# Next head's maxima and rows made in the middle of a head and carried through DRAM; routing in 16-bit floats with the gates kept in the gathered rows

## The chip, the cores and the metric

The kernel runs on one core of one Trainium2 chip. The metric is the time of one execution on the device in microseconds (us). Besides the span, which runs from the first to the last instruction of the profiled execution, there is the clock that TensorE was granted, as a share of full speed.

The core's engines work from queues of their own: TensorE (PE in the profile; PEld is its weight load), VectorE (DVE), ScalarE (ACT), GpSimd (POOL) and SyncE (SP, which issues most DMA transfers here). An engine takes its instructions in the order in which they stand in its queue. Semaphores order work between queues.

## The reference, cut to what matters

The input is 1250 nodes of 768 numbers and 41250 directed edges. Two blocks add to the input, each after a layer normalisation: the first is a graph network (two attention layers over the edges, and a linear combination) plus a linear attention (`mix`); the second is a mixture of eight experts, of which each node uses two.

```python
h = (x @ W).reshape(n, H, C)                      # layer 1: H=4, C=192; layer 2: H=2, C=96
s_src = (h * a_src).sum(-1); s_dst = (h * a_dst).sum(-1)
e = leaky_relu(s_src[src] + s_dst[dst], 0.2)
emax = segment_max(e, dst)
ee = exp(e - emax[dst])
alpha = ee / segment_sum(ee, dst)[dst]
out = segment_sum(alpha[:, :, None] * h[src], dst)
...
k = elu(x @ Wk + bk) + 1;  v = x @ Wv + bv        # mix, 12 heads of 64
kv = einsum('bhnd,bhne->bhde', k, v)              # and q likewise, then out @ Wo
...
gate = xt @ Wg + bg                               # 8 experts
scores, idx = top_k(gate, 2)
y = (gelu(xt @ W1[e] + b1[e])) @ W2[e] + b2[e]    # for each expert e
out = sum over a node's two experts of scores * y
```

## The kernel before, in words

Nodes are tiled as 10 tiles (NT) of 125 (PT). The edges are turned into a dense table `AT` of edge counts (source tile by destination) and a table `mask` of ones and zeros (destination tile by source). An attention head is then a dense job over 1250 x 1250 numbers.

**A head (`attend`, L496 to L538).** `ss` and `sd` are one column each of source and destination scores.

1. `across` (L498 to L508) turns a column of 10 x 125 scores into a row of 1250 that stands in all 125 partitions. It does ten TensorE transposes of a broadcast column (L504), four to a PSUM bank, and three ScalarE copies (L506). The first such row is `ss_row`, from which the least score of the head (`least`, L481 to L493) is taken off by the copy's bias, so that all entries are at least zero.
2. For each destination tile, one VectorE instruction multiplies `ss_row` with the mask and keeps the largest product (L515, `scr` and `top`): the largest neighbouring source score. Ten of these make a head's maxima.
3. L518 to L525 form from `top` the columns `up`, `dn` and `sl`. `up` and `dn` go through `across` to become `up_row` and `dn_row`.
4. For each source tile `st`, ScalarE takes two exponentials (L533 into `w`, L534 into `v`), VectorE takes the larger (L535) and limits and multiplies it with the edge counts (L536), and TensorE multiplies `w` with the features (`gather`): in layer 1 ten matmuls into `ag` (L548), in layer 2 three (L569). A matmul in 32-bit floats stands in the profile as two records.
5. In layer 1 the head ends with a reciprocal (L555) and ten VectorE instructions that add the scaled result into `h2` (L557). In layer 2 ScalarE copies the result out (L574). Layer 2 reads `h2`, so it begins when all four heads of layer 1 are added.

There are four heads in layer 1 and two in layer 2. The buffers that matter: three `w`, two `v`, one each of `ss_row`, `up_row` and `dn_row`, and one `ag`, which lies in five of the eight PSUM banks; `across` has one bank and the projection below has two.

**The key and value projection (L600 to L629)** depends on none of the heads. For each node tile and each half of 384 columns, there are six matmuls with Wk, six with Wv (L607), an exponential part on VectorE and ScalarE (L611 to L614), a copy (L617), three matmuls of keys by values (L621) and an addition to `kvacc` (L627, L629).

**What sets the order.** The kernel is written in a tile framework that schedules each engine's queue when the program is built: work that is ready by the framework's reckoning goes first in the order of the text, and later work fills the gaps. The order is fixed from then on. This is how the projection's matmuls come to stand between the heads' work on TensorE. The weights Wo, Wq and Wu (L584 to L591) take the place in memory of the graph's tables and so are loaded (L588, on SP) when the last head is done.

**Routing (L743 to L863).** For each node tile TensorE computes a query (L751), the sum of the linear parts (`po`, L781) and of the graph part (`u`, L792); VectorE adds and normalises (`xl`); the normalised row is written to `xl_d` in DRAM (L802); transposes and six matmuls give the eight gate values (L807, L810). VectorE ranks them (L817 to L826), two matmuls with a triangle and a matrix of ones count earlier nodes with the same expert (L830, reading `sel` and `cum`), and the result is a place in a list of 80 columns (NV) of 128 for each of the node's two experts. One-hot tables `hot` (L849) and `put` (L852, twice: node number and gate value) are multiplied into `inv` (L854), in 32-bit floats. At the end `idx` (node numbers, L859) and `gs` (gate values, L861) are read from `inv`.

**Experts (L899 to L984).** For each expert, three groups of 128 nodes are gathered from `xl_d` by an indirect DMA on GpSimd's queue (L909), transposed (L912, L915), passed through the two layers (L926, L938), scaled by the gates in `gs` (L942) and added to the output by an indirect DMA (L943). What does not fit in three groups follows in `other` (L959).

Of the kernel before, what the change touches and what calls it, by code (L numbers as in the profile page):

```python
# [54 lines left out]
FIX = 3  # L55
# [14 lines left out]
def gps_block(ctx: ExitStack, tc: tile.TileContext, x, src, dst, norm_g, norm_b, W1, a_src1, a_dst1,  # L70
# [60 lines left out]
    xl_d = dram.tile([N + 128, D], F32)  # L131
# [348 lines left out]
    def least(ss, H):  # L480

        mn = small.tile([PT, H], F32, name="mn")
        nc.vector.tensor_reduce(mn, ss.rearrange("p t h -> p h t"), AX.X, ALU.min)
        p = four()
        nc.tensor.transpose(p[:H, 0], mn, ident[:PT, :PT])
        m1 = small.tile([H, 1], F32, name="m1")
        nc.vector.tensor_reduce(m1, p[:H, 0], AX.X, ALU.min)
        p = four()
        nc.tensor.transpose(p[:, 0, :H], m1.to_broadcast([H, PT]), ident[:H, :H])
        lo = small.tile([PT, 2, H], F32, name="lo")  # L490
        nc.vector.tensor_copy(lo[:, 0], p[:, 0, :H])
        nc.vector.tensor_scalar(lo[:, 1], p[:, 0, :H], -1.0, None, op0=ALU.mult)
        return lo  # L493

    def attend(ss, sd, lo, wp, rb, gather):

        def across(cols, name, bufs, bias=0.0):

            row = rb.tile([PT, N], F32, name=name, bufs=bufs)
            for g0 in range(0, NT, 4):  # L500
                n = min(4, NT - g0)
                p = four()
                for q in range(n):
                    nc.tensor.transpose(p[:, q], cols[:, g0 + q:g0 + q + 1].to_broadcast([PT, PT]),  # L504
                                        ident[:PT, :PT])
                nc.scalar.activation(row[:, g0 * PT:(g0 + n) * PT],  # L506
                                     p[:, :n].rearrange("p a b -> p (a b)"), AF.Identity, bias=bias)
            return row  # L508


        ss_row = across(ss, "ss_row", 1, lo[:, 1:2])
        top = small.tile([PT, NT], F32, name="top")
        for t in range(NT):
            scr = wp.tile([PT, N], BF16, name="scr", bufs=1)
            nc.vector.tensor_tensor_reduce(scr, ss_row, mask[:, t], 1.0, 0.0, ALU.mult, ALU.max,  # L515
                                           top[:, t:t + 1])

        nc.vector.scalar_tensor_tensor(top, top, lo[:, 0:1], sd, op0=ALU.add, op1=ALU.add)  # L518
        nc.vector.scalar_tensor_tensor(top, top, SLOPE, top, op0=ALU.mult, op1=ALU.max)
        up = small.tile([PT, NT], F32, name="up")  # L520
        dn = small.tile([PT, NT], F32, name="dn")
        sl = small.tile([PT, NT], F32, name="sl")
        nc.vector.tensor_sub(up, sd, top)
        nc.vector.scalar_tensor_tensor(dn, sd, SLOPE, top, op0=ALU.mult, op1=ALU.subtract)
        nc.vector.tensor_scalar(sl, ss, SLOPE, None, op0=ALU.mult)  # L525
        up_row = across(up, "up_row", 1)
        dn_row = across(dn, "dn_row", 1)
        for st in range(NT):


            w = wp.tile([PT, N], F32, name="w", bufs=3)
            v = wp.tile([PT, N], F32, name="v", bufs=2)
            nc.scalar.activation(w, up_row, AF.Exp, bias=ss[:, st:st + 1])  # L533
            nc.scalar.activation(v, dn_row, AF.Exp, bias=sl[:, st:st + 1])  # L534
            nc.vector.tensor_tensor(w, v, w, op=ALU.max)  # L535
            nc.vector.scalar_tensor_tensor(w, w, 2.0, AT[:, st, :N], op0=ALU.min, op1=ALU.mult)  # L536
            gather(st, w)

    lo1 = least(s1[:, :, :, 0], H1)
    with tc.tile_pool(name="wp", bufs=3) as wp, tc.tile_pool(name="rb", bufs=1) as rb:  # L540
        with tc.tile_pool(name="ag_p1", bufs=1, space=PSUM) as ag_p:
            for hd in range(H1):
                ag = ag_p.tile([PT, NT // 2, 512], F32, name="ag")

                def gather1(st, w):
# [6 lines left out]
                attend(s1[:, :, hd, 0], s1[:, :, hd, 1], lo1[:, :, hd], wp, rb, gather1)  # L552
                v = ag[:, :, :2 * CG].rearrange("p a (b c) -> p a b c", b=2)
                rd = small.tile([PT, NT // 2, 2, 1], F32, name="rd")
                nc.vector.reciprocal(rd, v[:, :, :, C2:C2 + 1])  # L555
                for t in range(NT):
                    nc.vector.scalar_tensor_tensor(h2[:, t], v[:, t // 2, t % 2], rd[:, t // 2, t % 2],  # L557
                                                   h2[:, t], op0=ALU.mult, op1=ALU.add)
# [3 lines left out]
        lo2 = least(h2[:, :, at:at + H2], H2)  # L562
        with tc.tile_pool(name="ag_p2", bufs=1, space=PSUM) as ag_p:
            for hd in range(H2):
                ag = ag_p.tile([C2 + 1, 3, 512], F32, name="ag")

                def gather2(st, w):
# [4 lines left out]
                attend(h2[:, :, at + hd], h2[:, :, at + H2 + hd], lo2[:, :, hd], wp, rb, gather2)  # L572
                for i, (a, b) in enumerate(NCH):
                    nc.scalar.copy(o2T[:, hd, a:b], ag[:, i, :b - a])  # L574
# [23 lines left out]
    for t in range(NT):  # L598
        ky = kp.tile([PT, D], F32, name="ky", bufs=2)
        va = kp.tile([PT, KC, 129], F32, name="va")  # L600
        nc.gpsimd.memset(va[:, :, 128:], 1.0)
        for k in range(2):
            half = slice(k * 384, (k + 1) * 384)
            for w in (Wk_sb, Wv_sb):
# [4 lines left out]
                if w is Wk_sb:  # L609
                    ke = kp.tile([PT, 384], F32, name="ke", bufs=1)  # L610
                    nc.vector.tensor_add(ky[:, half], ps[:PT, :384], bk_b[:, half])  # L611
                    nc.vector.tensor_scalar(ke, ky[:, half], 0.0, None, op0=ALU.min)
                    nc.scalar.activation(ke, ke, AF.Exp)
                    nc.vector.scalar_tensor_tensor(ky[:, half], ky[:, half], 0.0, ke, op0=ALU.max,  # L614
# [5 lines left out]
            for c in range(3):  # L620
                nc.tensor.matmul(ps[:, c * 129:(c + 1) * 129],  # L621
                                 ky[:, (3 * k + c) * 128:(3 * k + c + 1) * 128], va[:, 3 * k + c],
# [63 lines left out]
    zero = fp.tile([128, D], F32)  # L686
    nc.gpsimd.memset(zero, 0.0)
    nc.sync.dma_start(xl_d[N:], zero)
    nc.sync.dma_start(out[N:], zero)
# [4 lines left out]
    gs = fp.tile([128, NV + 1], F32)  # L694
# [4 lines left out]
    with ExitStack() as rs:  # L699
# [7 lines left out]
        def numbers(shape, pattern, base, mult, name):  # L707
            t = rp.tile(shape, F32, name=name)
# [8 lines left out]
        row128 = numbers([PT, 128], [[1, 128]], 0, 0, "row128")  # L717
        steps = numbers([128, NE, NJ - FIX], [[0, NE], [128, NJ - FIX]], 128 * FIX, 0, "steps")
        slot_row = numbers([PT, NV], [[1, NV]], 0, 0, "slot_row")
# [6 lines left out]
        ones = rp.tile([PT, 128], F32)  # L726
        nc.gpsimd.memset(ones, 1.0)
        tri = rp.tile([PT, 128], F32)
# [4 lines left out]
        nc.gpsimd.memset(gs[:, NV:], 0.0)  # L733
# [5 lines left out]
        cum = rp.tile([PT, NT + 1, NE], F32)  # L739
        nc.vector.memset(cum[:, 0], 0.0)  # L740
        inv = g_p.tile([128, 2, NV], F32, name="inv", bufs=1)
# [26 lines left out]
        for t in range(NT):  # L768
# [30 lines left out]
            xl = rl.tile([PT, D], F32, name="xl")  # L799
            normalise(xl, xt)  # L800
            for p, tt in token_rows(t):
                nc.sync.dma_start(xlr[p, tt], xl[p])  # L802
# [6 lines left out]
            gate = rl.tile([PT, NE], F32, name="gate")  # L809
            nc.vector.tensor_add(gate, pg[:PT, :NE], bg_b)  # L810

# [11 lines left out]
            sel = rl.tile([PT, NE], F32, name="sel")  # L823
# [10 lines left out]
            two = rl.tile([PT, 2, 2, NE], F32, name="two")  # L834
            for i, a in enumerate((at, gate)):
                nc.vector.tensor_mul(two[:, i], kth, a[:, None, :].to_broadcast([PT, 2, NE]))
            both = rl.tile([PT, 2, 2], F32, name="both")
# [112 lines left out]
    for e in range(NE):  # L950
        hT = hidden(ring[e], xT, FIX, fb1T[:, :, e:e + 1])
        if e + 1 < NE:
            xT = gather([r for r, _ in fixed(e + 1)])
# [62 lines left out]
```

## Time and profile before

| | |
|---|---|
| time, median of 3 runs | 1179.41 us (1175.86 to 1180.65) |
| the profiled execution | 1180.66 us, span 1178.6 us |
| TensorE's granted clock over the span | 0.971 |
| busy: TensorE, weight load, VectorE, ScalarE, GpSimd | 1077.8, 723.6, 669.1, 358.1, 76.3 us |
| first L535 of layer 1, last L557 of layer 1 | 249.2 us, 466.2 us |
| first L535 of layer 2, last L569 | 503.0 us, 593.4 us |
| first L781 | 613.0 us |
| first gather (L909) | 937.5 us |

How the page is read. The busy time of an engine is the time in which one of its instructions ran. Matmuls are pipelined, so their time in the listing is longer than the distance between two of them. The chain is found by going back from the last instruction to what released it. A stretch of the span is shown as a line with its ends, its length, the busy time of each engine (with the number of instructions), the clock and the DMA engines' mean busy share and rate. A timeline shows merged instructions with start and duration, and in brackets the idle time before them and what ended it.

### The profile page before, as it was taken

The numbers are of one execution on the slowest core, as the hardware profiler recorded it, in microseconds if no ns is written. First come the engines' busy times: TensorE is split into PE (matmuls) and PEld (weight loads), VectorE is DVE, ScalarE is ACT, GpSimd is POOL, SyncE is SP. The second block draws the span as 40 slices with busy tenths as digits, with TensorE's granted clock in tenths as the row PEclk, the third lists the DMA queues.
The fourth block names the chain that finished last, engine by engine and source line by source line (L and its number), as shares of the span: only waits on it lengthen the run. The fifth ranks groups of instructions, "written<-read, shape, count | busy, mean of one in ns | idle before, by whom it ended". The sixth has DMA issues, their size and how long they took to land.

```text
span 1178.6 us, 12106 instructions
## 1 busy us (share of the span) xinstructions
PE 1077.8 (91%) x4583; PEld 723.6 (61%) x4583; DVE 669.1 (57%) x1366; ACT 358.1 (30%) x527; POOL 76.3 (6%) x100
## 2 busy tenths in 40 slices
PE   2599998999999999988989999999999589999993
PEld 2586655578788878544545666666666356666652
DVE  6866666669696966687922555555555422222210
ACT  2131114373737373373712211111111011111111
POOL 1000000000000000000000000000000122322321
PEclk9999998999999999989989999999999789999997
DMA  5014000000000001000083111111123537777533
GB/s 156 27 51 163 16 25 1 1 1 1 1 1 1 1 1 53 1 0 1 1 319 103 40 40 40 40 40 40 39 65 106 191 91 188 200 209 219 121 56 54
DMA packets 33282, 79.62 MB, mean 68 GB/s; under 512 B 5258, under 2 KB 13020, under 8 KB 33208
## 3 DMA queue, kind: packets, MB, share of 16 engines
q1 hardware_dynamic: 27608, 59.02, 15.2%
q0 software_dynamic: 5600, 19.66, 8.4%
q8 instruction: 40, 0.66, 0.2%
q14 instruction: 34, 0.28, 0.1%
HBM read 60.37 MB, written 18.30 MB: 67 GB/s over the span
## 4 chain that ended last, share of the span: by engine, by line
PE 70%; DVE 20%; DMA 5%; issue 2%; ACT 2%; POOL 1%; DVEq 0%; SPq 0%; POOLq 0%; ACTq 0%
PE po L781 13%; PE ph L926 8%; PE py L938 7%; PE mm L430 7%; PE mm L607 7%; PE mm L751 7%; DVE scr L515 6%; DVE w L535 5%; DVE w L536 5%; PE ag L548 3%; PE ag L569 2%; PE u L792 2%; PE px L912 2%; PE mm L405 2%; DMA w<-in_L_gnn_Wu_dram 2%
## 5 line engine op out<-in xcount | busy, mean ns | idle before, releaser
L548 PE MATMUL ag<-kept,w 125*125 125x198 f32 x800 | 137.4, 333 | 5.1 <-DVE w L536 4.9
L548 PEld LDWEIGHTS ag<-kept,w 125*125 125x125 f32 x800 | 133.5, 188 | 9.0 <-DVE w L536 9.0
L926 PE MATMUL ph<-xsT,w 128*128 128x384 f32 (+1 forms) x324 | 100.6, 470 | 1.8 <-DVE xsT L915 1.8
L938 PE MATMUL py<-w,hT 128*128 128x384 f32 x300 | 100.6, 486 | 0.0
L430 PE MATMUL mm<-Wg,xnT 128*125 128x400 f32 x240 | 91.8, 520 | 1.0 <-DVE xnT L321 0.6
L607 PE MATMUL mm<-Wv_sb,xnT 128*125 128x384 f32 x240 | 85.7, 489 | 4.8 <-DVE kvacc L627 4.8
L535 DVE TENSOR_TENSOR w<-v,w 125x1250 f32<-125x1250 f32 x60 | 86.3, 1453 | 6.6 <-ACT w L533 5.9
L515 DVE CUSTOM_DVE_ANT_0 scr<-ss_row,mask 125x1250 bf16<-125x1250 f32 x60 | 87.2, 1453 | 0.5 <-ACT ss_row L506 0.2
L781 PE MATMUL po<-w,xnT 128*125 128x384 f32 x240 | 84.8, 496 | 2.6 <-DMA w<-in_L_gnn_Wu_dram 2.6
L536 DVE SCALAR_TENSOR_TENSOR w<-w,AT 125x1250 f32<-125x1250 f32 x60 | 86.4, 1455 | 0.4
L926 PEld LDWEIGHTS ph<-xsT,w 128*128 128x128 f32 x324 | 59.8, 193 | 41.4 <-DVE xsT L915 2.4
L607 PE MATMUL mm<-Wk_sb,xnT 128*125 128x384 f32 x240 | 84.4, 486 | 0.0
L534 ACT ACTIVATE v<-dn_row,sl 125x1250 f32<-125x1250 f32 x60 | 79.3, 1333 | 16.9 <-DVE w L535 16.4
L751 PE MATMUL mm<-w,xnT 128*125 128x384 f32 x240 | 84.2, 489 | 0.0
L915 DVE COPY xsT<-px 128x384 f32<-128x384 f32 x50 | 25.5, 552 | 99.2 <-PE px L912 77.3
L781 PE MATMUL po<-w,qT 128*125 128x384 f32 x240 | 80.8, 486 | 0.0
L938 PEld LDWEIGHTS py<-w,hT 128*128 128x128 f32 x300 | 55.3, 190 | 33.9
L941 DVE TENSOR_TENSOR ys<-py,wb 128x768 f32<-128x768 f32 x25 | 23.9, 958 | 74.0 <-PE py L938 45.5
L781 PEld LDWEIGHTS po<-w,xnT 128*125 128x125 f32 x240 | 44.2, 190 | 30.1 <-DMA w<-in_L_gnn_Wu_dram 2.8
L781 PEld LDWEIGHTS po<-w,qT 128*125 128x125 f32 x240 | 44.2, 188 | 29.4
L607 PEld LDWEIGHTS mm<-Wv_sb,xnT 128*125 128x125 f32 x240 | 42.4, 187 | 31.1 <-DVE kvacc L627 6.9
L751 PEld LDWEIGHTS mm<-w,xnT 128*125 128x125 f32 x240 | 43.6, 188 | 27.6 <-ACT qT L321 0.2
(274 smaller groups left out, 1415.6 us busy)
## 6 DMA issues: line engine op xcount, KB each, us to landing
w<-in_L_ffn_W_dram SPq DMA_DIRECT2D x18, 1152.0 KB
xt<-in_x_dram SPq DMA_DIRECT2D x20, 336.0 KB
wb<-in_L_ffn_b_dram SPq DMA_DIRECT2D x9, 384.0 KB
out_dram<-xt SPq DMA_DIRECT2D x10, 336.0 KB
xl_d<-xl SPq DMA_DIRECT2D x10, 336.0 KB
W_sb<-in_L_gnn_W_dram SPq DMA_DIRECT2D x1, 2304.0 KB
Wk_sb<-in_L_mix_Wk_dram SPq DMA_DIRECT2D x1, 2304.0 KB
Wv_sb<-in_L_mix_Wv_dram SPq DMA_DIRECT2D x1, 2304.0 KB
```

Source lines behind the costliest of these rows:

```text
L430: nc.tensor.matmul(ps[:PT, :2 * (CG + 2)], xnT[:, c, t * PT:(t + 1) * PT], Wg1[:, c, 2 * k:2 * k + 2].rearrange("p h c -> p (h c)"), start ...
L515: nc.vector.tensor_tensor_reduce(scr, ss_row, mask[:, t], 1.0, 0.0, ALU.mult, ALU.max, top[:, t:t + 1])
L534: nc.scalar.activation(v, dn_row, AF.Exp, bias=sl[:, st:st + 1])
L535: nc.vector.tensor_tensor(w, v, w, op=ALU.max)
L536: nc.vector.scalar_tensor_tensor(w, w, 2.0, AT[:, st, :N], op0=ALU.min, op1=ALU.mult)
L548: nc.tensor.matmul(ag[:, t // 2, o:o + CG], w[:, t * PT:(t + 1) * PT], gw[:, st, hd], start=st == 0 and t % 2 == 0, stop=st == NT - 1, ski ...
L607: nc.tensor.matmul(ps[:PT, :384], xnT[:, c, t * PT:(t + 1) * PT], w[:, c, half], start=c == 0, stop=c == KC - 1)
L751: nc.tensor.matmul(ps[:PT, :384], xnT[:, c, tk], Wq_sb[:, c, half], start=c == 0, stop=c == KC - 1)
L781: nc.tensor.matmul(po[k][:, :384], l, r[:, k * 384:(k + 1) * 384], start=i == 0, stop=i == len(parts) - 1)
L915: nc.vector.tensor_copy(xT[:, 3 * a:3 * a + 3, j * 128:(j + 1) * 128], px[:, a, :384].rearrange("p (b n) -> p b n", b=3))
L926: nc.tensor.matmul(ph[:, :n * 128], w[0][:, o:o + 128], xT[:, c, :n * 128], start=c == 0, stop=c == KC - 1)
L938: nc.tensor.matmul(py[:, k, :384], hT[:, f, j * 128:(j + 1) * 128], w[:, o:o + 384], start=f == 0, stop=f == FC - 1)
```

## The change

*Attention.* `attend` becomes `layer`, which takes all heads of a layer. The least score of each head is subtracted from its column by VectorE (`over`), and the columns of all heads are turned by one transpose (`to_rows`), copied by ScalarE and written to DRAM. The rows of the layer's first head are still made by `across`; those of the other heads are read back from DRAM by a DMA that repeats a row in all 125 partitions. What was `up_row` and `dn_row` is one buffer `row` of two rows, of which there are two; `v` has one buffer instead of two. The call for the next head's `ss_row`, maxima and rows (`sides_of`) stands after the third source tile of a head instead of at the start of the next.

*Projection.* The buffer `ky` holds a half (384) instead of a whole tile, and there are three.

*Routing.* `row128`, `slot_row`, `ones`, `tri`, `cum`, `sel`, `hot` and `put` are 16-bit floats. `put` and `inv` hold node numbers alone, so that one L852 of two is left and `inv` has 80 columns instead of 160. The eight gate values of a node are kept as eight more columns of `xl`, and two more DMAs for each tile write them to `xl_d`, whose rows are 776 numbers long.

*Experts.* A gather brings the gates along, and the scaling reads them from the gathered row (`xg`, six buffers instead of three). In `other` the gate column is copied after the gather, by an address in a register.

```diff
+    row_d = [dram.tile([n * NT, PT], F32, name=f"row{i}") for i, n in enumerate((H1, H2, 2))]
-    xl_d = dram.tile([N + 128, D], F32)
+    xl_d = dram.tile([N + 128, D + NE], F32)
...
-        ss_row = across(ss, "ss_row", 1, lo[:, 1:2])
...
+    def to_rows(cols, d):
+        n = cols.shape[1]
+        p = four()
+        nc.tensor.transpose(p[:n, 0], cols, ident[:PT, :PT])
+        r = small.tile([H1 * NT, PT], F32, name="r", bufs=2)
+        nc.scalar.copy(r[:n], p[:n, 0])
+        nc.sync.dma_start(d, r[:n])
...
+    def layer(ss, sd, H, d, wp, rb, head):
+        lo = least(ss, H)
+        over = small.tile([PT, H, NT], F32, name="over", bufs=1)
+        for h in range(H):
+            nc.vector.tensor_scalar(over[:, h], ss[:, :, h], lo[:, h:h + 1], None, op0=ALU.subtract)
+        to_rows(over.rearrange("p h t -> p (h t)"), d)
+        def sides_of(h):
+            ss_row = rb.tile([PT, N], F32, name="ss_row")
+            if h:
+                nc.sync.dma_start(ss_row, row_bcast(d[h * NT:(h + 1) * NT], PT))
+            else:
+                across(over[:, h], ss_row)
...
+            row = rb.tile([PT, 2, N], F32, name="row", bufs=2)
+            if h:
+                to_rows(sides.rearrange("p a t -> p (a t)"), row_d[2])
+                nc.sync.dma_start(row.rearrange("p a n -> p (a n)"), row_bcast(row_d[2], PT))
+            else:
+                for a in range(2):
+                    across(sides[:, a], row[:, a])
+            return row, sl
+        ahead = sides_of(0)
+        for h in range(H):
+            row, sl = ahead
+            gather, finish = head(h)
+            for st in range(NT):
+                if st == 3 and h + 1 < H:
+                    ahead = sides_of(h + 1)
+                w = wp.tile([PT, N], F32, name="w", bufs=3)
+                v = wp.tile([PT, N], F32, name="v", bufs=1)
...
-        ky = kp.tile([PT, D], F32, name="ky", bufs=2)
+                    ky = kp.tile([PT, 384], F32, name="ky", bufs=3)
...
-        ones = rp.tile([PT, 128], F32)
+        ones = rp.tile([PT, 128], F16)
...
-        inv = g_p.tile([128, 2, NV], F32, name="inv", bufs=1)
+        inv = g_p.tile([128, NV], F32, name="inv", bufs=1)
...
-            xl = rl.tile([PT, D], F32, name="xl")
+            xl = rl.tile([PT, D + NE], F32, name="xl")
...
-            gate = rl.tile([PT, NE], F32, name="gate")
+            gate = xl[:, D:]
             nc.vector.tensor_add(gate, pg[:PT, :NE], bg_b)
+            for p, tt in token_rows(t):
+                nc.sync.dma_start(xlr[p, tt, D:], gate[p])
...
-                put = rl.tile([PT, 2, NV], F32, name="put")
-                for i, v in enumerate((node1[:, t:t + 1], both[:, 1, k:k + 1])):
-                    nc.vector.tensor_scalar(put[:, i], slot_row, s_f[:, 0, k:k + 1], v,
-                                            op0=ALU.is_equal, op1=ALU.mult)
+                put = rl.tile([PT, NV], F16, name="put")
+                nc.vector.tensor_scalar(put, slot_row, s_f[:, 0, k:k + 1], node1[:, t:t + 1],
+                                        op0=ALU.is_equal, op1=ALU.mult)
...
-            xg = sp.tile([128, D], F32, name="xg", bufs=3)
+            xg = sp.tile([128, D + NE], F32, name="xg", bufs=6)
...
+        if isinstance(e, int):
+            gates = xg[:, D + e:D + e + 1]
+        else:
+            gates = sp.tile([128, 1], F32, name="gates")
+            nc.vector.tensor_copy(gates, xg[:, bass.ds(e + D, 1)])
         nc.scalar.mul(ys, ys, gates)
```

## The prediction

> **What bounds the kernel now.** I read the page first, then the stretches of the attention part, the timelines of VectorE and TensorE there, and last the clock and the DMA rate at three spots.
>
> ```profile
> PE 1077.8 (91%) x4583; PEld 723.6 (61%) x4583; DVE 669.1 (57%) x1366; ACT 358.1 (30%) x527; POOL 76.3 (6%) x100
> ...
> PE 70%; DVE 20%; DMA 5%; issue 2%; ACT 2%; POOL 1%; DVEq 0%; SPq 0%; POOLq 0%; ACTq 0%
> ```
>
> TensorE is busy 91% of the span and carries 70% of the chain. The stretches show where it is not full (columns: us, then busy us of PE, PEld, DVE, ACT, POOL, then PE clock, DMA share, GB/s):
>
> ```profile
> 249.20:466.20 217.00, 206.07 (x1093) 178.44 (x1092) 179.20 (x224) 116.52 (x117) 2.13 (x4) 1.00 0.02 8
> 466.20:503.00 36.80, 34.71 (x141) 21.43 (x139) 22.87 (x47) 12.99 (x21) 0.22 (x2) 1.00 0.00 1
> 503.00:593.40 90.40, 83.34 (x273) 44.08 (x272) 76.97 (x80) 54.94 (x56) 0.22 (x2) 0.96 0.00 0
> 593.40:613.00 19.60, 15.39 (x65) 9.21 (x64) 6.49 (x21) 5.22 (x18) 2.40 (x13) 0.97 0.97 376
> 613.00:920.00 307.00, 306.98 (x1125) 187.15 (x1125) 153.24 (x411) 55.01 (x89) 0.50 (x4) 0.99 0.20 65
> 920.00:949.00 29.00, 13.56 (x53) 9.79 (x52) 13.60 (x62) 1.14 (x3) 5.20 (x6) 0.60 0.56 173
> ```
>
> Rows one to three are layer 1's heads, the passage between the layers, and layer 2's heads. TensorE is nearly full there although each head's softmax is VectorE work, because the scheduler fills its gaps with the key/value projection (L607, L621), which depends on none of it. Routing (613 to 920) is TensorE alone. So an attention that ends sooner pays only so far as TensorE work is removed or TensorE idles less. Three timelines give the unit prices:
>
> ```profile
> 258.81 1.45 DVE L535 TENSOR_TENSOR w<-v,w 125x1250 f32<-125x1250 f32 x1
> 260.18 1.45 DVE L515 CUSTOM_DVE_ANT_0 scr<-ss_row,mask 125x1250 bf16<-125x1250 f32 x1
> 261.56 0.08 DVE L515 DVE_READ_ACCUMULATOR2_ANT top<- 125x1 f32 x1
> 261.56 1.46 DVE L536 SCALAR_TENSOR_TENSOR w<-w,AT 125x1250 f32<-125x1250 f32 x1
> ```
>
> Already in the old kernel the next head's maxima (`scr`) stand among this head's weights: max, `scr`, product start 1.37 to 1.38 apart, 4.12 us a step, or 2.74 without `scr`.
>
> ```profile
> 428.71 33.77 PE L548 MATMUL ag<-kept,w 125*125 125x198 f32 x200 [1.28 <-DVE w L536]
> ...
> 551.17 1.46 PE L607 MATMUL mm<-Wv_sb,xnT 128*125 128x384 f32 x4
> 552.47 0.60 PE L504 MATMUL rb<-ident,up 125*125 125x125 f32 x4
> ...
> 597.97 4.04 PE L607 MATMUL mm<-Wk_sb,xnT 128*125 128x384 f32 x12
> 601.85 4.03 PE L607 MATMUL mm<-Wv_sb,xnT 128*125 128x384 f32 x12
> 606.45 0.94 PE L621 MATMUL mm<-va,ky 125*128 125x129 f32 x6 [0.57 <-ACT va L617]
> ```
>
> A head of layer 1 is 33.8 us of matmuls, 3.4 a step: less than VectorE's 4.12, more than its 2.74. Half a token tile of key/value work is 3.87+3.87+0.67 (L621 back to back) = 8.41 us. Four row transposes (552.47 to 552.90) cost 0.44, 0.11 each.
>
> **Attention, part by part.** 120 of the 180 row transposes go (30 in each of the four heads that are not a layer's first): 120 x 0.11 = 13 us of TensorE, and 36 row copies of ScalarE, which was 54% busy and off the path. Six small transposes come (under 1 us). The order of the changed kernel's instructions shows what else moves. Layer 1's four heads now follow each other with only ten projection matmuls and three small ones among their 400, where the old order had two halves (16.8 us) at each of three boundaries. After layer 2's last head eight halves are left; before, one. The same work is done; the question is how long TensorE idles meanwhile. I shift the old times stretch by stretch.
>
> *First head.* The first weight was at 249.2. The subtraction of the least (four 0.08 us operations and a small transpose in front of the rows) adds 0.7. Five maxima of head 1 now precede the first weight on VectorE's queue, and their row comes by DMA into a buffer that head 0's maxima free at about 237.5. The nearest transfer is a bias copied to 125 partitions:
>
> ```profile
> 458.00:458.50 0.50, 0.50 (x5) 0.50 (x4) 0.00 (x0) 0.00 (x0) 0.00 (x0) 1.00 0.33 135
> 460.50:461.00 0.50, 0.50 (x5) 0.50 (x4) 0.00 (x0) 0.00 (x0) 0.50 (x1) 1.00 0.83 301
> ```
>
> The first line is such a copy, at a third of the DMA engines and about 127 GB/s over its 3 us; the second is a copy to 128 partitions. Issue to use was 455.87 to 460.3, 4.45 us for 384 KB, so 1.43 fixed. A 625 KB row takes 1.43+4.92 = 6.35 us and lands at 244.0. Five maxima at 1.5 and two projection operations (0.47 each) put the first weight at 252.5: +3.3. At 301 GB/s it would be +1; that is the lower end.
>
> *Layer 1 from there.* VectorE sets heads 0 and 1: 20 steps x 2.74 + 20 `scr` x 1.39 + 3.5 (L555, ten L557) + 1.4 small = 87.5. One `ag` buffer serves all heads, so at a boundary TensorE waits from its last matmul until ten L557 are done: by VectorE's queue 5.5 us. Does that drop its clock?
>
> ```profile
> 506.00:508.00 2.00, 0.72 (x1) 0.40 (x2) 2.00 (x2) 2.00 (x4) 0.00 (x0) 0.54 0.00 0
> ...
> 510.00:512.00 2.00, 2.00 (x4) 0.85 (x3) 1.46 (x1) 0.20 (x1) 0.00 (x0) 0.50 0.00 0
> 512.00:514.00 2.00, 2.00 (x5) 0.80 (x4) 0.83 (x1) 2.00 (x2) 0.00 (x0) 0.75 0.00 0
> ```
>
> Yes: after some 4 us nearly idle before 507 the clock stood at half for 6.1 us, 3.05 us lost. With three `w` buffers VectorE absorbs a part: I take 2 us at each of two boundaries (ends 0 and 3). The Trainium skill ("TensorE: Matmul & The Clock Gate", Part 1) puts the way back at one busy window of 3.4 us, so, as an estimate, 1.7 us lost, which VectorE's slack would nearly hide; by it the sum would be about 4 us less. From head 1's last weight on I add the queues by hand: head 2's boundary 9, five steps with the rest of head 3's maxima to 25, then TensorE's 3.4 a step to 46.5, ten projection matmuls (6.5), head 3 (34.3), L555 and L557 (3.7): 91. In all 87.5+91+4 = 182.5, against 217.0: **-34.5**.
>
> *The later rows.* From a head's sides to the next head's first exponential VectorE's order leaves 19, 17 and 15 us (heads 1, 2, 3), more in layer 2. The round trip is 0.6 for transpose and copy, a write of 20 rows (no such write is shown; the small load on the chain took 2.2, the scattering writes 5.6 to 5.95; I take 2.5, being as small as the first), and 1.43 + 1250/127 = 11.3: 14.4. Hidden; at the upper end 17.8, one head is late by 1 to 3 us. On SP the write stands behind the next `ss_row` load, which waits for maxima that end before the sides, and no weight load is behind it until attention is over.
>
> *Passage.* As before, plus `ss_row` by DMA ahead of five maxima: the maxima end 25.1 after layer 1 does, the row lands 6.4 later, five maxima and two projection operations take 8.3: first weight after 39.8 instead of 36.8: **+3.0**.
>
> *Layer 2.* With one `v` buffer a step is max 1.45 + exponential 1.33 + two hand-overs of 0.06 = 2.9, if ScalarE does the other exponential meanwhile (ends 2.74 and, if not, 4.12). 20 x 2.9 + 5 x 1.39 + 3 + 2.4 for the last matmuls = 70.5, against 90.4: **-19.9**.
>
> *The rest of the projection.* Before: 593.4 to 612.97, where `Wu` lands 18.4 us after its issue, and 3.2 more, since the clock stands at half until 619: 22.8. After: 4.0 as before 597.2, 0.7, eight halves (67.3), two gaps of 0.6, the transposes at L644 and what stands among them 4.2, six L781 matmuls put into the other gaps (3.9), less nine L781 done ahead (5.8): 75.5, and the weights' 18.4 are covered by it. **+52.7**.
>
> Sum: +3.3 -34.5 +3.0 -19.9 +52.7 = **+4.6 us**, in spite of the transposes: attention ends 48 us sooner, but TensorE has idled 15 us more.
>
> **Routing.** Per tile four f32 passes at L854 (0.67 us back to back at 912.9) and four at L830 (0.48) become two 16-bit passes each. Nearest row:
>
> ```profile
> L465 PE MATMUL pm<-identb,some 125*125 125x125 bf16 x100 | 9.0, 239 | 0.0
> ```
>
> 0.09 each: 1.15 - 0.35 = 0.8 a tile (ends: 0.5 if a pass costs as much as at L854, 0.95 at half of L465). Nine tiles lie under full TensorE: **-7.2**. In the tenth all of it is on the chain to the first gather, at half clock: L854 1.56 to 0.5, L830 1.0 to 0.45, L867 0.3, two L852 0.46 and L861 0.15 less: **-2.4**. The ten tiles' gate writes (20 DMAs, 32 bytes a row) stand on SP ahead of the next tile's `xt` and, at the end, of the weights of L658 for the fourth expert, wanted some 100 us later. The last gates are ready at 928.8 and, at 0.8 us of issue and 2.2 to 5.95, land by 935.6; the gather would start at 935.1. Nothing to 0.5, I take nothing. The Trainium skill ("DMA: Bandwidth & Descriptors", Specifications) warns that writes below 512 B are read-modify-write; no row prices that. Experts: same order, TensorE full, the 32 bytes more a row are hidden; 0.
>
> **Sum.** +4.6 -7.2 -2.4 = -5.0. The profiled execution took 1180.66 us (1178.6 span), 1.25 over the median of 1179.41. Forecast 1180.66 - 5.0 - 1.25 = 1174.4.
>
> **Rivals.** *A, cheaper stalls:* no half clock at the boundaries (-4), steps of 2.74 (-3), rows at 301 GB/s (-5): 1174.4 - 12 = 1162; for it, the 530-to-540 stretch, 55% busy at full clock; against, 507 above. *B, the whole gain stays:* the eight halves hide and 48 us are won, 1179.4 - 48 - 10 = 1121. Only the 18.4 us of `Wu` could hide them; against it, TensorE's 306.98 of 307 behind. *C, slower, by the broadcast:* long rows move slower than 127 GB/s. Each us on `ss_row` costs two; the sides have 5 and 3 us of slack at heads 1 and 2. At 80 GB/s: 2 x 2.9 + 0.8 + 2.8 = 9.4, 1184; at 63, half, 2 x 5 + 5 + 7 + 4 = 26, 1200. It decides (over 1185.3) from some 77 GB/s down. Against it, four such copies at 125 to 129. *D, slower, by one `v` buffer:* steps of 4.12 without `scr`: 15 in layer 1 at +0.7, 15 in layer 2 at +1.2, 28 us, 1203; half of it 1188. *E, nothing is moved:* half true already (`scr`), but the order differs; about 1170, routing alone.
>
> **Chances.** Forecast 0.55 (1168 to 1182), A 0.14, E 0.06, B 0.02, C 0.12, D 0.11. Within 0.5% is 1173.5 to 1185.3, about what a measurement tells from no change. Faster: 0.20 of the forecast's and A, E and B almost whole: 0.41; same: 0.33 and 0.03 of C and D; slower 0.23. Range 1162 to 1190.
>
> **What would show it.** Right: layer 1 near 183 us with TensorE some 30 us idle; first weight near 252 behind an `ss_row` of 6 us; half clock after two boundaries; 75 us of L607 after the last head; a routing tile of 28.7 instead of 29.5 (734.2 to 763.7 on the chain). Wrong: row waits ahead of exponentials, steps of 4 us in layer 2, or projection matmuls not late.

## The result, and the profile after

The changed kernel takes 1208.64 us (median of 6, 1204.51 to 1210.55) against 1179.53 (6 runs beside it): ratio 1.0247, 95% interval 1.022 to 1.0273. The forecast was 1174.4, range 1162 to 1190. The profiled execution took 1209.09 us, span 1207.4, 28.8 more than before's 1178.6.

TensorE's busy line of the page after:

```profile
PE 1070.5 (89%) x4428; PEld 712.1 (59%) x4428; DVE 666.3 (55%) x1339; ACT 345.5 (29%) x497; POOL 77.2 (6%) x99
```

TensorE has 7.3 us less busy time in a span 28.8 us longer. The stretches of the kernel after (us, then busy us of PE, PEld, DVE, ACT, POOL, then clock, DMA share, GB/s):

```profile
251.50:430.20 178.70, 156.63 (x843) 148.52 (x844) 164.36 (x196) 101.85 (x83) 1.92 (x2) 0.94 0.10 38
430.20:471.20 41.00, 37.21 (x145) 22.35 (x143) 29.65 (x59) 13.41 (x22) 0.11 (x1) 1.00 0.04 16
471.20:543.90 72.70, 63.33 (x186) 31.28 (x187) 67.24 (x65) 49.37 (x43) 0.11 (x1) 0.93 0.05 18
543.90:629.70 85.80, 83.47 (x301) 49.24 (x299) 21.37 (x52) 12.25 (x32) 3.31 (x19) 1.00 0.35 123
629.70:701.80 72.10, 68.30 (x225) 38.82 (x226) 29.57 (x61) 16.20 (x30) 0.00 (x0) 0.95 0.16 44
701.80:923.60 221.80, 221.80 (x836) 135.58 (x835) 115.96 (x320) 38.91 (x59) 0.00 (x0) 1.00 0.20 62
923.60:953.70 30.10, 13.29 (x52) 8.82 (x50) 14.11 (x59) 1.24 (x3) 5.94 (x6) 0.60 0.57 184
953.70:1146.00 192.30, 174.51 (x587) 105.22 (x588) 37.11 (x57) 30.32 (x40) 46.48 (x36) 0.96 0.57 146
```

The last row is new: among the experts TensorE stands still for 17.8 of 192.3 us. Before, nearly the same length from the first expert matmul on has it busy throughout, at a clock of 0.99 instead of 0.96, which is by estimate another 6 us (192 x 0.03):

```profile
949.13:1141.40 192.27, 192.27 (x671) 116.17 (x672) 41.99 (x64) 34.83 (x46) 52.38 (x41) 0.99 0.64 160
```

Stage by stage, with the terms of the prediction split at the same points. The prediction's +52.7 and the first tile's share of routing (-0.8) are one figure:

| stage | before | after | change | predicted |
|---|---|---|---|---|
| start to the first weight | 249.2 | 251.5 | +2.3 | +3.3 |
| layer 1 | 217.0 | 178.7 | -38.3 | -34.5 |
| passage | 36.8 | 41.0 | +4.2 | +3.0 |
| layer 2 | 90.4 | 72.7 | -17.7 | -19.9 |
| rest of the projection, to the products with Wo (L683, after L722) | 26.4 | 85.8 | +59.4 | |
| first tile of routing | 70.8 | 72.1 | +1.3 | +51.9 with the row above |
| the other tiles, to the last u matmuls | 228.0 | 221.8 | -6.2 | -6.4 |
| from there to the first expert matmul (L926, after L963) | 30.5 | 30.1 | -0.4 | -2.4 |
| experts | 229.5 | 253.7 | +24.2 | 0 |
| sum | 1178.6 | 1207.4 | +28.8 | -5.0 |

Three terms were off: 24.2 in the experts, 8.8 in the projection with the first tile, 2.0 before the first gather.

**The experts.** TensorE's order is the same in both kernels there. What differs is GpSimd's queue, which issues the gathers (`xg`) and the scatters that add to the output (`out_dram`). Its timeline before, and then after, from the first expert's first scatter on:

```profile
963.99 0.94 POOL L909 DMA_INDIRECT xg<-xl_d,idx  x1 [14.29 <-PE px L912]
966.00 0.94 POOL L909 DMA_INDIRECT xg<-xl_d,idx  x1 [1.06 <-PE px L912]
968.01 0.94 POOL L909 DMA_INDIRECT xg<-xl_d,idx  x1 [1.07 <-PE px L912]
971.27 1.61 POOL L943 DMA_INDIRECT out_dram<-ys,idx  x1 [2.32 <-ACT ys L942]
977.92 1.57 POOL L943 DMA_INDIRECT out_dram<-ys,idx  x1 [5.04 <-DMA out_dram<-ys,idx]
989.16 1.55 POOL L943 DMA_INDIRECT out_dram<-ys,idx  x1 [9.66 <-ACT hT L928]
```

```profile
975.40 1.61 POOL L985 DMA_INDIRECT out_dram<-ys,idx  x1 [25.82 <-ACT ys L984]
977.32 1.00 POOL L945 DMA_INDIRECT xg<-xl_d,idx  x1 [0.30 <-PE py L975]
981.85 1.59 POOL L985 DMA_INDIRECT out_dram<-ys,idx  x1 [3.53 <-DMA out_dram<-ys,idx]
983.75 1.00 POOL L945 DMA_INDIRECT xg<-xl_d,idx  x1 [0.30 <-issue]
992.94 1.60 POOL L985 DMA_INDIRECT out_dram<-ys,idx  x1 [8.20 <-issue]
994.84 0.99 POOL L945 DMA_INDIRECT xg<-xl_d,idx  x1 [0.31 <-issue]
```

Before, the third expert's gathers are issued ahead of the first expert's scatters. After, each stands behind one of them. A scatter waits for the one before it to land (`<-DMA out_dram`; the profile does not name this for every one), so three scatters are 6.5 and 11.1 us apart, and the gathers with them. On TensorE, after:

```profile
992.34 0.82 PE L948 MATMUL px<-ident,xg 128*128 128x128 f32 x6
994.32 0.85 PE L948 MATMUL px<-ident,xg 128*128 128x128 f32 x6
1000.12 0.85 PE L948 MATMUL px<-ident,xg 128*128 128x128 f32 x6 [3.66 <-DMA xg<-xl_d,idx]
1000.80 10.89 PE L975 MATMUL py<-w,hT 128*128 128x384 f32 x28
```

The third transposes wait 3.66 us for the gather issued at 994.84. The `py` matmuls behind them take 10.89 us instead of the 9.20 that they take in the kernel before; behind a shorter wait, 2.76 us at 1030.02, they take 9.20 here too. This recurs: from the second expert on, the distance from one expert's first matmul to the next one's is 28.2 to 31.1 us five times over, where it was 25.3 (976.60 to 1001.91, for one).

The trace also shows with what the long landing of the second scatter coincides. During these five experts SyncE issues the loads of a later expert's weights, the first of them from 980.93 on; from 981.85 to 992.94 the DMA engines are busy for 0.92 of the time, at 291 GB/s. The last of these loads is issued at 1103.49. From 1127 on, two scatters of the same expert are 6.3 to 8.0 us apart, and the expert that begins at 1132.28 takes 26.1 us. That the loads are what delays the scatter was not tried.

**Why the order changed.** The gate is now a column of `xg`, so ScalarE reads `xg` in the scaling (L984), at an expert's end. Before, `xg` was free once transposed. With six buffers, the seventh gather (the third expert's first) cannot be issued before the first scaling, and the scheduler put it behind the scatter that follows this scaling.

### The profile page after: what moved, and what is told of

It is laid out like the page before. It is cut to its first block, busy times and chain, and to the rows that moved or that the text cites. A ratio compares the mean times of both kernels' runs of the same rounds, so it can differ in the third digit from the quotient of the medians.

```text
span 1207.4 us, 11865 instructions
## 1 busy us (share of the span) xinstructions
PE 1070.5 (89%) x4428; PEld 712.1 (59%) x4428; DVE 666.3 (55%) x1339; ACT 345.5 (29%) x497; POOL 77.2 (6%) x99
## 5 line engine op out<-in xcount | busy, mean ns | idle before, releaser
L579 PE MATMUL ag<-kept,w 125*125 125x198 f32 x800 | 146.5, 346 | 22.9 <-DVE w L567 12.4
L579 PEld LDWEIGHTS ag<-kept,w 125*125 125x125 f32 x800 | 141.8, 197 | 27.5 <-DVE w L567 16.1
L975 PE MATMUL py<-w,hT 128*128 128x384 f32 x300 | 105.3, 504 | 0.0
L963 PE MATMUL ph<-xsT,w 128*128 128x384 f32 (+1 forms) x324 | 100.2, 469 | 1.7 <-DVE xsT L951 1.7
L565 ACT ACTIVATE v<-row,sl 125x1250 f32<-125x1250 f32 x60 | 80.0, 1333 | 42.1 <-DVE w L566 41.8
L819 PE MATMUL po<-w,xnT 128*125 128x384 f32 x240 | 84.3, 494 | 0.0
L963 PEld LDWEIGHTS ph<-xsT,w 128*128 128x128 f32 x324 | 59.5, 193 | 41.1 <-DVE xsT L951 2.4
L819 PE MATMUL po<-w,qT 128*125 128x384 f32 x240 | 80.8, 487 | 0.0
L975 PEld LDWEIGHTS py<-w,hT 128*128 128x128 f32 x300 | 57.8, 199 | 36.4 <-issue 4.5
L564 ACT ACTIVATE w<-row,s 125x1250 f32<-125x1250 f32 x40 | 53.5, 1337 | 34.7 <-PE ag L579 34.6
L819 PEld LDWEIGHTS po<-w,qT 128*125 128x125 f32 x240 | 44.1, 188 | 29.5 <-issue 0.2
```

The costliest lines, as they stand in the source:

```text
L564: nc.scalar.activation(w, row[:, 0], AF.Exp, bias=ss[:, st, h:h + 1])
L565: nc.scalar.activation(v, row[:, 1], AF.Exp, bias=sl[:, st:st + 1])
L579: nc.tensor.matmul(ag[:, t // 2, o:o + CG], w[:, t * PT:(t + 1) * PT], gw[:, st, hd], start=st == 0 and t % 2 == 0, stop=st == NT - 1, ski ...
L819: nc.tensor.matmul(po[k][:, :384], l, r[:, k * 384:(k + 1) * 384], start=i == 0, stop=i == len(parts) - 1)
L963: nc.tensor.matmul(ph[:, :n * 128], w[0][:, o:o + 128], xT[:, c, :n * 128], start=c == 0, stop=c == KC - 1)
L975: nc.tensor.matmul(py[:, k, :384], hT[:, f, j * 128:(j + 1) * 128], w[:, o:o + 384], start=f == 0, stop=f == FC - 1)
```

## The experiments

Ratios are to the kernel before, run beside each. The theories and rivals that the expectations name by letters (H and C; W, A and B) belong to the experiments; they are not the prediction's rivals A to E.

**1. Gates copied out at once.** VectorE copies the gate column after the transposes, and the scaling reads the copy; three `xg` buffers as before:

```diff
-            xg = sp.tile([128, D + NE], F32, name="xg", bufs=6)
+            xg = sp.tile([128, D + NE], F32, name="xg", bufs=3)
...
-            xgs.append(xg)
+            g = sp.tile([128, 1], F32, name="gates", bufs=6)
+            nc.vector.tensor_copy(g, xg[:, D + e:D + e + 1] if isinstance(e, int) else
+                                  xg[:, bass.ds(e + D, 1)])
+            xgs.append(g)
```

> The changed kernel, but the gate column is copied out of the gathered row into a small tile right after the transposes, and xg has its three buffers of before; rows stay 3104 bytes long. Theory H (the gathered tile is held until the scaling, so that from the seventh on each gather stands between two scatters on GpSimd's queue and the third of an expert comes late): an expert takes 25.3 us again instead of 30.8, the experts' stage 229.5 instead of 253.7, time 1208.6 - 24.2 = 1184 us, ratio to the kernel before about 1.004. Rival W (the longer, no longer 512-byte-aligned rows make gathers slow): an expert stays near 30 us and the time near 1208. Rival A (the loss comes from when attention and the weight loads end, not from the gathers): also near 1208.

Measured: 1182.39 us, 1.0027 (1.0016 to 1.0038). TensorE in this kernel, two experts following each other:

```profile
1080.17 11.77 PE L966 MATMUL ph<-xsT,w 128*128 128x384 f32 x36
1091.78 0.82 PE L948 MATMUL px<-ident,xg 128*128 128x128 f32 x6
...
1105.48 1.78 PE L966 MATMUL ph<-xsT,w 128*128 128x384 f32 x5
```

25.31 us again, with rows of 3104 bytes. The row's length is not the cause (rival W), nor is the later attention (rival A).

**2. The hold alone, in the kernel before.**

```diff
-            xg = sp.tile([128, D], F32, name="xg", bufs=3)
+            xg = sp.tile([128, D], F32, name="xg", bufs=6)
...
         nc.scalar.mul(ys, ys, gates)
+        last = sp.tile([128, 1], F32, name="last")
+        nc.scalar.activation(last, ys[:, :1], AF.Identity, bias=xg[:, :1])
```

> The kernel before, rows of 3072 bytes and gates in gs, with six xg buffers and one small ScalarE operation after the scaling that reads one column of xg, so that the tile is held exactly as in the changed kernel. Theory H: TensorE waits 3 to 4 us for each expert's third gather, an expert takes some 31 us instead of 25.3, time 1179.5 + 24 = about 1204 us, ratio 1.02. Rival W (row length) and rival A (attention): no change but 25 ScalarE operations of 0.2 us off the path, 1180 us.

Measured: 1206.23 us, 1.0245 (1.0212 to 1.0278). TensorE in this kernel, third transposes of three experts:

```profile
994.87 0.84 PE L913 MATMUL px<-ident,xg 128*128 128x128 f32 x6 [4.34 <-DMA xg<-xl_d,idx]
...
1024.99 0.84 PE L913 MATMUL px<-ident,xg 128*128 128x128 f32 x6 [2.99 <-DMA xg<-xl_d,idx]
...
1053.79 1.51 PE L913 MATMUL px<-ident,xg 128*128 128x128 f32 x6 [3.35 <-DMA xg<-xl_d,idx]
```

In this trace the experts take 256.2 us from the first expert matmul on (946.00), 26.7 more than before. The hold by itself costs at least what the experts lost (24.2), without the attention, the 16-bit floats or longer rows.

**3. Is it the hold, or the place in the queue?** After's trace shows that the buffer was not what the gather waited for: ScalarE's scaling that frees it began at 982.17 and took 0.94, and the gather was issued at 994.84:

```profile
982.17 0.94 ACT L984 ACTIVATE ys<-ys,xg 128x768 f32<-128x768 f32 x1 [3.18 <-DVE ys L978]
```

So the gather call was moved, in the text, from the next expert's loop to just ahead of the scatter (`fetch` issues one gather); gates are still read from the held row:

```diff
         nc.scalar.mul(ys, ys, gates)
+        if then is not None:
+            xgs.setdefault(e + 2, []).append(fetch(then))
         nc.gpsimd.indirect_dma_start(out, bass.IndirectOffsetOnAxis(rows, 0), ys, None,
```

> The changed kernel, gates still read from the held row, six buffers; on GpSimd's queue alone each later gather stands one place further forward, ahead of the scatter that it stood behind (seven gathers, then scatter and gather in turn); the order on the other four engines is the same. Theory H as refined by the traces (it is not the buffers that are too few, but the scatter in front, which waits until the scatter before it has landed): the third gather of an expert is issued some 10 us earlier, TensorE no longer waits for it, 1208.6 - 24 = 1184 us. Rival B (six held buffers are too few whatever the order): an expert stays above 29 us, 1200 us or more.

Measured: 1185.42 us, 1.0053 (1.0037 to 1.007). GpSimd's timeline and TensorE's in this kernel:

```profile
980.07 1.00 POOL L942 DMA_INDIRECT xg<-xl_d,idx  x1 [1.01 <-ACT ys L986]
984.03 1.59 POOL L989 DMA_INDIRECT out_dram<-ys,idx  x1 [2.97 <-DMA out_dram<-ys,idx]
985.93 0.99 POOL L942 DMA_INDIRECT xg<-xl_d,idx  x1 [0.30 <-issue]
994.98 1.60 POOL L989 DMA_INDIRECT out_dram<-ys,idx  x1 [8.06 <-PE px L951]
```

```profile
997.14 0.84 PE L951 MATMUL px<-ident,xg 128*128 128x128 f32 x6
```

The third gather is issued at 985.93 instead of 994.84, ahead of the scatter, and no wait stands at its transposes. An expert takes 25.3 us again, with a single wait of 0.35 us (at 1073.55). The hold cost time through the place that it gave the gathers in the queue, not by the number of buffers; the experiments' rival B falls. The 3 us by which this kernel is slower than that of experiment 1 were not followed up; experiment 6 shows 1.5 us that six buffers cost before the first expert.

**4. Attention alone.** The kernel before with the hunks of `attend`/`layer` and `ky` only:

```diff
-    def attend(ss, sd, lo, wp, rb, gather):
+    def layer(ss, sd, H, d, wp, rb, head):
...
-        ky = kp.tile([PT, D], F32, name="ky", bufs=2)
+                    ky = kp.tile([PT, 384], F32, name="ky", bufs=3)
```

> The kernel before with the changed attention and the changed key buffer alone; routing and experts as before. By the trace of the changed kernel, the first tile of routing ends 11.3 us later than before with 0.8 us of 16-bit savings in it: +12 us, 1191.6 us, ratio 1.010. By the prediction's own sum for attention (+4.6): 1184, ratio 1.004. If the old order of the experts' gathers is not touched by a later attention (theory H), an expert stays at 25.3 us; by rival A it becomes longer and the time goes above 1200.

Measured: 1191.96 us, 1.011 (1.0087 to 1.0132), so +10 to +16 us where the prediction had +4.6. An expert takes 25.3 us in its trace (988.37 to 1013.68), so a later attention alone does not slow the experts. The first tile of routing stands still as in the changed kernel: 3.77 us at the first query's transposes, which experiment 7 takes up.

**5. Routing alone.** The kernel before with the hunks of routing and gates, and the gate copy and three buffers of experiment 1:

```diff
-                put = rl.tile([PT, 2, NV], F32, name="put")
+                put = rl.tile([PT, NV], F16, name="put")
...
-            gate = rl.tile([PT, NE], F32, name="gate")
+            gate = xl[:, D:]
```

> The kernel before with the changed routing alone (16-bit floats, gates carried by the rows of 3104 bytes), the gates copied out of the gathered row at once and three xg buffers. Theory H: nine tiles at 0.78 us less each and 0.4 in the tail, experts as before: 1179.5 - 7.4 = 1172 us, ratio 0.994. By the prediction's own sum (7.2 + 2.4): 1170. Rival W: the rows cost some 24 us, near 1196.

Measured: 1166.33 us, 0.99 (0.9879 to 0.9921), a gain of 9 to 14 us, above the expected 7.4. Between the first weight and the end its trace is 10.7 us shorter than before's: 0.8 up to the end of the first tile, 6.3 in the others, 2.1 before the first expert matmul (28.46 against 30.56), 1.5 in the experts. The rest of the 12 lies ahead of the first weight, where the traces of before and of experiment 2, alike up to routing, also differ (249.2 and 245.4). What that part gained, if anything, stays open.

**6. Three buffers or six.** The gate copy with six buffers kept, against experiment 1:

```diff
-            xg = sp.tile([128, D + NE], F32, name="xg", bufs=3)
+            xg = sp.tile([128, D + NE], F32, name="xg", bufs=6)
```

> The changed kernel with the gate column copied out at once, six xg buffers kept. Theory H: an expert takes 25.3 us with six buffers as with three; about 1184 us. On the first gather: if six buffers overlay a tile that routing still reads (its last transposes), it starts some 1.5 to 1.9 us later after the last u matmul than with three, as in the changed kernel; if it waits for the gate's write to DRAM, it starts late with three as well, which the first run already speaks against.

Measured: 1182.11 us (a single run). The first transposes, first in this kernel, then in that of experiment 1:

```profile
946.00 1.51 PE L948 MATMUL px<-ident,xg 128*128 128x128 f32 x6 [5.12 <-DMA xg<-xl_d,idx]
```

```profile
943.56 1.51 PE L948 MATMUL px<-ident,xg 128*128 128x128 f32 x6 [3.59 <-DMA xg<-xl_d,idx]
```

From the last u matmuls to the first expert matmul it is 30.1 us with six buffers and 28.6 with three, gates written to DRAM in both. Experiment 2 agrees, with six buffers and no gate write: 5.04 us of wait, and 32.1 us (913.92 to 946.00) where the kernel before has 30.5. So the gate write is not what delays the first gather; the number of buffers is. That the additional buffers lie over a tile that routing reads last was argued from the layout and not tried by itself.

**7. The first tile.** After attention ends, the weights land while the projection runs, and nine of the `po` matmuls with `xnT` (L781, after L819) are done ahead. TensorE before, and then after, around the first query:

```profile
630.75 7.36 PE L751 MATMUL mm<-w,xnT 128*125 128x384 f32 x22
637.94 5.97 PE L781 MATMUL po<-w,xnT 128*125 128x384 f32 x18
...
644.46 0.86 PE L319 MATMUL mm<-ident,qy 125*128 125x125 f32 x6
...
645.80 7.91 PE L751 MATMUL mm<-w,xnT 128*125 128x384 f32 x24
```

```profile
647.97 1.45 PE L819 MATMUL po<-w,xnT 128*125 128x384 f32 x4
649.26 1.46 PE L830 MATMUL u<-Wu_sb,kept 96*125 96x384 f32 x4
654.48 1.51 PE L320 MATMUL mm<-ident,qy 125*128 125x125 f32 x6 [3.76 <-DVE qy L800]
655.92 10.01 PE L789 MATMUL mm<-w,xnT 128*125 128x384 f32 x24
```

Before, nine `po` matmuls and one u matmul filled the time that VectorE needs for the query, and the transposes waited for nothing. After, two `po` and two u matmuls were left for it: 3.76 us idle, and the transposes and the next 24 records took 2.8 us more than the same ones before (0.86 and 7.91). To test it, the second tile's query is written ahead of the first one's transposes, in the kernel of experiment 1:

```diff
-        qT_next = query(0)
+        qys = [query(0), query(1)]
+        qT_next = turned(qys[0])
```

> The kernel of the first run (changed kernel, gate column copied out, three xg buffers), but the second tile's query matmuls are written ahead of the first query's transposes, so that they stand between them on TensorE. Theory C (the nine linear matmuls done ahead during the projection were the cover of the first query's 6 us on VectorE; without them TensorE waits 3.8 us and its clock falls to half, another 2.8): both go, 1182.4 - 6.5 = 1176 us. Rival (the 8 us that the first tile lost come from elsewhere, say from late xt loads or the linear sums): within 1.5 us of 1182.

Measured: 1174.22 us, 0.9964 (0.995 to 0.9979). TensorE in this kernel:

```profile
640.90 15.10 PE L789 MATMUL mm<-w,xnT 128*125 128x384 f32 x46
655.84 0.49 PE L320 MATMUL mm<-ident,qy 125*128 125x125 f32 x3
```

Both queries run in one piece and the transposes follow without a gap: 8.2 us gained by the medians, 7.4 by the ratios, and 7.4 in the traces from the first L722 to the first expert matmul (322.6 and 315.2 us). With this and experiment 1 the changed kernel is just faster than before.

**8 and 9. The same on the old attention.** On the kernel of experiment 5, `Wu` is loaded first (8), and then the second query is also put ahead (9):

```diff
-    Wo_sb, Wq_sb, Wu_sb = weight(Wo), weight(Wq), weight(Wu[:D])
+    Wu_sb, Wo_sb, Wq_sb = weight(Wu[:D]), weight(Wo), weight(Wq)
```

> The routing-only kernel with the weight Wu loaded before Wo and Wq instead of after. Theory C seen from the other side, on the old attention: the 2.8 us wait for Wu and the half clock behind it (3.2) go, but the linear matmuls then run ahead and the first query is uncovered: TensorE waits some 4 to 5 us at its transposes and loses 2.8 by the clock. 1166.3 - 6 + 7 = 1167, within 3 us. Rival (running ahead is a plain gain): 1166.3 - 6 = 1160.

> Wu first and the second query ahead of the first query's transposes, on the routing-only kernel. Theory C: the wait for Wu is gone and the first query stays covered, 1166.3 - 6 = 1160 us, ratio to the kernel before 0.984. Rival: like the run with Wu first alone.

Measured: 1169.65 us, 0.992 (0.9899 to 0.9941), and 1162.45 us, 0.9844 (0.982 to 0.9867). TensorE in the kernel of experiment 8:

```profile
606.23 5.32 PE L780 MATMUL po<-w,xnT 128*125 128x384 f32 x16
...
639.30 1.51 PE L319 MATMUL mm<-ident,qy 125*128 125x125 f32 x6 [5.69 <-DVE qy L761]
640.75 10.31 PE L750 MATMUL mm<-w,xnT 128*125 128x384 f32 x24
```

The matmuls run ahead at 606, where TensorE used to wait for `Wu`, and the wait is back at 639 with 5.69 us: no gain. Only with the query covered as well does the gain show. It is 3.9 us by the medians. From the first weight to the end the traces of experiments 5, 8 and 9 take 918.7, 921.3 and 910.8 us, a gain of 7.9; but in the kernel of experiment 9 the first weight comes at 249.8 us, in that of 5 at 243.6, though their text is the same up to there. What moves that part was not found. Experiment 9 is the fastest kernel found, 1.6% faster than before, with the old attention.

## Why the prediction was wrong

**Experts, "same order, TensorE full, the 32 bytes more a row are hidden; 0": failed, +24.2.** The order was the same on TensorE alone. The step did not go through GpSimd's queue, nor ask until when `xg` is now held. Before's timeline had what was needed: scatters 6.7 and 11.2 us apart, each behind the landing of the one before, and TensorE without slack. The 32 bytes were hidden indeed (experiments 1 and 5), and the gates in rows need not cost anything. Experiments 2 and 3 show the mechanism from both sides. None of the prediction's rivals named it.

**Rest of the projection, "less nine L781 done ahead (5.8)": failed, 8.8 with the first tile.** The eight halves, the order and the landing of the weights came as said. But the credit was taken as if these nine matmuls were on the path, while in the old order they covered the first query's 6 us on VectorE. Removing them moved nothing forward, and the uncovered wait came with 2.8 us at a lower clock: 5.8 not gained and 2.8 lost, less 0.6 for the second u matmul that now stands in the gap. From the end of the first query's matmuls to the first `po` matmuls with the query it was 15.6 us (637.94 to 653.54) and is 17.8 (647.97 to 665.77), +2.2 instead of -5.8: 8.0 of the 8.8. Experiment 7 got 7.4 to 8.2 back, and 8 and 9 show the same on the old attention. The working names what hides each cost, but did not ask what the work taken as a gain had itself been hiding.

**Tail, -2.4: nearly right for three buffers, -0.4 with six.** 28.6 and 28.5 us with three buffers (experiments 1 and 5) against 30.5 are -1.9 and -2.0. The six buffers were not reckoned with. The gate's DMA, taken at nothing, cost nothing visible.

**First head, +3.3: +2.3 in the profile, inside what the part ahead of it varies** (243.6 to 249.8 us in five kernels with the old attention), so the runs do not settle this term. VectorE waited for `ss_row` as said:

```profile
243.39 1.46 DVE L533 CUSTOM_DVE_ANT_0 scr<-ss_row,mask 125x1250 bf16<-125x1250 f32 x1 [5.29 <-DMA ss_row<-row]
```

Issued at 236.1, it was used 7.3 us later; 6.35 was reckoned with.

**Layer 1, -34.5: -38.3.** The boundary stall is there with the length given:

```profile
302.47 9.72 PE L579 MATMUL ag<-kept,w 125*125 125x198 f32 x39 [5.27 <-DVE h L588]
```

```profile
306.00:308.00 2.00, 2.00 (x8) 2.00 (x7) 2.00 (x4) 0.53 (x1) 0.00 (x0) 0.50 0.00 0
308.00:310.00 2.00, 2.00 (x12) 2.00 (x11) 1.37 (x3) 0.96 (x1) 0.00 (x0) 0.89 0.00 0
...
349.80:352.00 2.20, 2.20 (x7) 2.20 (x8) 2.20 (x2) 0.00 (x0) 0.00 (x0) 0.50 0.03 7
352.00:354.00 2.00, 2.00 (x11) 2.00 (x10) 2.00 (x4) 1.34 (x1) 0.00 (x0) 0.80 0.00 0
```

At the first boundary the clock was at half up to 308 and beyond, some 6 us. At the second (from 349.80 on) the stall was again 5.27, and full speed was back after some 3 us. The mean granted clock over the layer was 0.94. The Trainium skill ("TensorE: Matmul & The Clock Gate", Part 1) has at least one busy window of about 3.4 us and calls the window free-running: the second boundary's 3 us are about one window, the first's 6 are more than one.

The 3.8 us are the balance of two errors. Up to head 1's last weight (345.0) the layer took 93.5 us where 91.5 was reckoned, and from there 85.2 where 91 was. TensorE stood idle for 22.1 us, not for the 30 that were named as a sign of being right.

**Passage +3.0 and layer 2 -19.9: +4.2 and -17.7.** Both terms were about right. VectorE did wait for `v` in layer 2, by 0.37 to 1.06 us at a time, which the 2.9 us a step had only in part.

**Routing, -7.2 over nine tiles: right**, -6.2 over eight in the profile. The prediction's rivals B (the whole gain stays) and C (a slow broadcast) did not come; what the broadcast and `v` cost stayed within the sums. D's 28 us (one `v` buffer) were not there either.

Had the two failed steps and the tail come as written, the sum would have been right within 1.2 us (-5.0 against 28.8 - 24.2 - 8.8 - 2.0 = -6.2). That this is so close is in part luck: layer 1 came 3.8 us better, the passage and layer 2 together 3.4 worse.

## What to carry to other kernels

When a change makes a later instruction read a buffer, follow the buffer: who refills it, what now stands in front of the refill on the issuing queue, and what that waits for. An unchanged TensorE order says nothing about this, and moving the issue one place forward can cure it without giving up the change.

Work that is done early is a gain only if it was on the path; if it filled another engine's latency, its removal uncovers that latency, so name the filler that is left before taking credit.

## What the runs showed of the hardware

- A gather that stood behind one waiting scatter was issued 11.7 us after its buffer came free (983.1 to 994.84): on GpSimd's queue the gather did not pass it.
- The three scatters of an expert follow at unequal distances in both kernels: 6.65 and 11.24 us before, 6.45 and 11.09 after, for the first expert. The Trainium skill ("DMA: Bandwidth & Descriptors", Rules for kernel authors) asks an accumulating DMA to wait for the earlier one on the same bytes, which the traces show as the wait between scatters; the longer waits fall with the weight loads (DMA engines busy 0.92 of the time, 291 GB/s, from 981.85 to 992.94), and whether these are the cause was not tried.
- Gathers of 3104-byte rows cost no measurable time against 3072: 25.3 us an expert and a median of 4.9 us from issue to landing with both (experiment 1 and before).
- 5.27 us of TensorE idleness was followed by some 6 us at half clock at one boundary of layer 1 and by some 3 at the next.
